# Strassen's scheme in the first half of layer 0 of a two-layer graph network

## The chip, the core and the metric

The kernel runs on one core of one Trainium2 chip. The metric is device time in microseconds for one execution. The kernel before takes 1528.7 us, the median of three runs (1527.5 to 1532.0).

The engines are called as in the profile: PE is TensorE (PEld its weight loads), DVE is VectorE, ACT is ScalarE, POOL is GpSimd, and SP is SyncE, which here only issues transfers. ACT and POOL issue transfers as well. Every engine takes its instructions in the order in which the program lists them.

## The reference

Two layers work on 2048 nodes, a batch of 8 and 64 features, all in fp32. Cut to what matters:

```python
# layer 0
w  = einsum('nd,dkio->nkio', embedding, weight)       # weights of each node
As = [I, A, 2*A@A - I]
x_g = einsum('knm,bmc->bnkc', stack(As), x)
x  = layernorm(x + einsum('bnki,nkio->bno', x_g, w) + b)
# layer 1: the same with supports I, A, 2*A@A - I and
apt = softmax(relu(E @ E.T), axis=1)
x  = layernorm(x + ...)
```

A is a dense 2048 x 2048 matrix. The products with A are computed as u = A x and then z = A u, on a right-hand side of 2048 rows and 8 x 64 = 512 columns. Each node has its own 64 x 64 weights, made from its embedding.

## The kernel before

The work is cut into 40 stages: five phases of eight blocks, a block being 256 nodes. Phase A0 makes u = A x for layer 0 and applies the weights to the features [x; u]. Phase B0 makes z = A u and ends layer 0 with its normalisation. A1, Z1 (the softmax support) and V1 do the same for layer 1. Stage n is block n mod 8 of phase n div 8, so A0 is stages 0 to 7, B0 stages 8 to 15, A1 stages 16 to 23.

A stage's own part is its product (`product`, line 410). All the rest is fed in between the product's matrix instructions: each `put(n, place, f, ...)` (line 657) says that f is to be issued in stage n at a place from 0 to 64, scaled to the stage's length (64 units for a plain stage, 56 for a Strassen stage). The loop at line 751 walks through the products and issues what has come due. So the order on each engine is written by hand, and a stage n + 1 carries work that belongs to stage n: making its weights on PE (`weights`, line 306, tiles `pw`, in bursts of two or three groups), copying them out of PSUM into `w` on ACT and DVE (`copy`), transposing u (`turn`, line 395, tile `pt`), applying the weights to the features (`apply`, line 327, tile `po`, followed by updates of `acc` on DVE), and storing the result (`post`, line 356).

Products come in two kinds. A plain one (`straight`, line 435, tile `pu`, in A0 and A1) streams the block's 256 rows of A in four pieces of 512 KB and issues 32 matrix instructions of 128 rows by 512 columns. A Strassen one (`strassen`, line 455, tiles `p1` to `p7`, shown as `p`) cuts the block's rows of A and the right-hand side into quarters and makes seven products of quarter size, eight matrix instructions of 256 columns each. Its left operands are three quarters of A and four sums of quarters (`lefts`, line 246); its right operands are three quarters of the right-hand side and four sums T1 to T4 of them (`Sums`, line 609), which DVE makes once in a phase.

Before the change, A0 is plain in all eight blocks, and B0, A1 and V1 are plain in block 0 alone (`plain`, line 215). While A0 runs, DVE makes the four sums of quarters of A for blocks 1 to 7 out of the streamed pieces (`sums_of_a`, line 555) and SP stores them to DRAM (`sd`); the later phases read them from there.

A0's u stays in `u_all` in SBUF, from where B0 reads it. The same room holds the raw first weights at the start (line 128), and in A1 the four right-hand sums T1 to T4.

Buffers that the change touches: `stream` has four buffers of 512 KB for pieces of A, filled in order by SP through `Ahead` (line 217), which asks for a new piece as soon as fewer than four are ready. There are two PSUM accumulators (`ps_acc`), handed out in turn, so a product can start once all readers of the product before the last are done. Three more PSUM tiles (`ps_big`) are handed out in turn to `pw`, `pb`, `pt` and `po`. `wst` (three buffers) holds split weights, filled by SP. `wraw`, `wsplit`, `sq` and `row` are single buffers with several users.

## Time and profile before

| | |
|---|---|
| median of three runs | 1528.7 us |
| the profiled execution's own time | 1533.8 us |
| its span, first to last instruction | 1532.0 us |
| PE busy | 1497.5 us |
| DVE busy | 889.3 us |
| ACT busy | 455.0 us |
| POOL busy | 184.4 us |
| moved by transfers | 274.95 MB, 179 GB/s on average |

In the profile's tables a group is written `out<-in`, by the program's names without buffer numbers, then its shape, its count, its busy time and the mean length of one instruction, and last the idle time of the engine just ahead of it with what ended that idle time. All lines of the kernel's own instructions are shown as L42, because one helper issues them; groups are told apart by their tiles. Every fp32 matrix instruction appears as two PE records. Records of PE overlap a little, so the mean length of one is longer than the distance between two; the chain of work, which counts each moment once, gives the distance.

### The profile page before, as it was taken

The page shows a single profiled execution, that of the slowest core. Times are in us where ns is not written, and L with a number is a line of the kernel's source. Part 1 is how long each engine was busy: PE and PEld are TensorE (multiplying, and loading weights), DVE is VectorE, ACT ScalarE, POOL GpSimd, SP SyncE. Part 2 cuts the span into 40 slices and gives each one's busy share as a digit, 9 for nine tenths or more (in the row PEclk, how much of TensorE's full clock was granted, in tenths as well). Part 3 has the DMA queues.
Part 4 walks back from the last instruction along what each step waited for, and adds up shares of the span by engine and source line. Part 5 has one row for each costly group of instructions (what it writes and reads, how often), then busy time and mean ns, then how long its engine had stood idle before and what let it go on. Part 6 is the DMA issues. An engine that isn't in the chain of part 4 may idle for free.

```text
span 1532.0 us, 30543 instructions
## 1 busy us (share of the span) xinstructions
PE 1497.5 (98%) x13114; PEld 1147.6 (75%) x13114; DVE 889.3 (58%) x1600; ACT 455.0 (30%) x578; POOL 184.4 (12%) x303
## 2 busy tenths in 40 slices
PE   8999999999999999989999999999999999999996
PEld 3444444457899999567777777788888888888885
DVE  2766666656566666766666666543433366666665
ACT  0333223222221112154444444411111133333332
POOL 4201011110111111111111111010000000000100
PEclk9999999999999999999999999999999999999998
DMA  9777787763576656588788877823211346665661
GB/s 347 240 240 212 234 253 249 230 219 115 179 224 226 196 192 199 157 152 210 192 168 192 207 206 202 166 79 100 66 38 42 88 131 195 196 198 194 197 197 51
DMA packets 93511, 274.95 MB, mean 179 GB/s; under 512 B 13632, under 2 KB 30016, under 8 KB 91776
## 3 DMA queue, kind: packets, MB, share of 16 engines
q1 hardware_dynamic: 65120, 180.38, 41.0%
q0 software_dynamic: 22784, 78.98, 17.9%
q10 hardware_dynamic: 5472, 13.63, 2.5%
q8 instruction: 104, 1.70, 0.4%
q14 instruction: 31, 0.25, 0.1%
HBM read 212.08 MB, written 56.64 MB: 175 GB/s over the span
## 4 chain that ended last, share of the span: by engine, by line
PE 77%; issue 14%; DMA 4%; DVE 3%; POOL 2%; ACT 0%; SPq 0%; POOLq 0%; ACTq 0%; DVEq 0%
PE p L42 24%; PE pz L42 18%; PE pu L42 13%; PE po L42 11%; PE pw L42 7%; PE pt L42 1%; DMA wst<-wd 1%; DMA x<-in_x 1%; PE ps L42 1%; DVE acc L42 1%; PE pr L42 1%; DMA u<-in_w 1%; DVE w L42 1%; POOL x1d L42 1%; POOL t L42 0%
## 5 line engine op out<-in xcount | busy, mean ns | idle before, releaser
L42 ACT ACTIVATE w<-pw 128x1024 f32<-128x1024 f32 x304 | 296.3, 1021 | 301.1 <-PE pw L42 301.0
L42 DVE SCALAR_TENSOR_TENSOR acc<-po,mask,acc 128x256 f32<-128x256 f32 (+1 forms) x640 | 247.2, 426 | 91.1 <-PE po L42 80.8
L42 DVE COPY w<-pw 128x1024 f32<-128x1024 f32 x144 | 176.2, 1224 | 188.5 <-PE pw L42 187.7
L42 PE MATMUL pu<-x,a 128*128 128x512 f32 x576 | 268.5, 609 | 5.8 <-DMA x<-in_x 3.4
L42 PE MATMUL pz<-p,x 128*128 128x256 f32 x1024 | 232.7, 380 | 0.0
L42 PE MATMUL p<-a,u 128*128 128x128 f32 x1792 | 219.4, 278 | 4.6 <-DVE temps L42 4.6
L42 PEld LDWEIGHTS p<-a,u 128*128 128x128 f32 x1792 | 206.5, 192 | 15.8 <-DVE temps L42 5.7
L42 PE MATMUL po<-w,t 128*32 128x256 f32 (+1 forms) x5120 | 207.6, 338 | 7.7 <-issue 4.1
L42 PEld LDWEIGHTS pz<-p,x 128*128 128x128 f32 x1024 | 189.3, 190 | 24.2 <-issue 0.6
L42 PEld LDWEIGHTS pu<-x,a 128*128 128x128 f32 x576 | 104.8, 192 | 121.5 <-issue 106.3
L42 PEld LDWEIGHTS po<-w,t 128*32 128x32 f32 (+1 forms) x5120 | 127.5, 108 | 83.6 <-issue 18.4
L42 PEld LDWEIGHTS pw<-e,wst 64*128 64x128 f32 x1728 | 112.0, 184 | 58.2 <-issue 35.4
L42 PE MATMUL pw<-e,wst 64*128 64x256 f32 x1728 | 145.8, 296 | 2.1 <-ACT w L42 1.1
L42 DVE SCALAR_TENSOR_TENSOR p<-ps,c 128x512 f32<-128x512 f32 x64 | 44.2, 691 | 120.4 <-PE ps L42 120.1
L42 PE MATMUL p<-u,a 128*128 128x256 f32 x448 | 112.3, 388 | 0.0
L42 ACT ACTIVATE p<-p 128x512 f32<-128x512 f32 x64 | 40.2, 630 | 181.9 <-DVE p L42 181.9
L42 PEld LDWEIGHTS p<-u,a 128*128 128x128 f32 x448 | 81.0, 190 | 16.2 <-issue 2.9
L42 PE MATMUL p<-a,x 128*128 128x128 f32 x672 | 84.7, 279 | 0.0
L42 PE MATMUL p<-x,a 128*128 128x256 f32 x336 | 81.2, 383 | 0.0
L42 PE MATMUL p<-a,w 128*128 128x128 f32 x672 | 81.1, 279 | 0.0
L42 PEld LDWEIGHTS p<-a,x 128*128 128x128 f32 x672 | 78.2, 192 | 3.7
L42 PEld LDWEIGHTS p<-a,w 128*128 128x128 f32 x672 | 78.2, 195 | 1.8 <-issue 1.6
(108 smaller groups left out, 1106.3 us busy)
## 6 DMA issues: line engine op xcount, KB each, us to landing
wst<-wd SPq DMA_DIRECT2D x108, 512.0 KB, 5.4
a<-sd SPq DMA_DIRECT2D x84, 512.0 KB, 6.2
a<-in_adj_q SPq DMA_DIRECT2D x63, 512.0 KB, 4.0
a<-in_adj_b SPq DMA_DIRECT2D x40, 512.0 KB, 6.3
sd<-sums SPq DMA_DIRECT2D x28, 512.0 KB, 3.3
bx<-bx POOLq DMA_DIRECT2D x32, 256.0 KB, 7.8
acc<-bx POOLq DMA_DIRECT2D x16, 512.0 KB, 5.9
pd<-acc POOLq DMA_DIRECT2D x16, 512.0 KB, 4.9
```

Source lines behind the costliest of these rows:

```text
L42: return self._tc.keep_in_program_order(f(*args, **kwargs))
```

## The change

In phase A0, blocks 2 to 7 are made with Strassen's scheme. Block 0 and block 1 stay plain.

The left operands of these six stages are made where they lie. The stage takes the four quarters A11, A22, A21 and A12 into the four `stream` buffers, holds them (`held`), and DVE writes each sum over a quarter that is no longer needed; a buffer is given back after p7, p6, p5 and p3. POOL stores each sum to `sd` for the later phases, in place of `sums_of_a` and SP's stores, which only block 1 keeps.

The seven products come in another order in all phases: p1, p4, p7, p2, p6, p5, p3 instead of p1, p2, p4, p6, p5, p7, p3, with two more additions on DVE.

The right-hand sums T1 to T4 for A0 are made in stage 1 in `u_all`. So u no longer stays there: each stage of A0 stores its u to DRAM (`ud`) from POOL, and SP loads it back into `u_all` at the end of stage 7 as the T's are used up, block 7 in stage 8.

Around these: the start loads 13 slabs of x instead of 10 ahead of the first raw weights and the last three ahead of the second; the first weight splits move to later places; the warm-up multiplies 7 times 128 columns instead of 5 times 512; raw weights are loaded into `sq` and split into `row`, at later places; in A0, two of 16 `w` copies go to DVE instead of five; B0's last two posts move a little; block 7's x is reloaded from one place; the last stage applies the weights in another order.

The diff, cut to its core:

```diff
-    for c, slabs in enumerate((range(10), range(10, 13), range(13, NJ), ())):
+    for c, slabs in enumerate((range(13), range(13, NJ), (), ())):
...
-    for _ in range(5):
-        pe.matmul(ps[:, 0, :], idle[:, 0:P], idle, start=True, stop=True)
+    for _ in range(7):
+        pe.matmul(ps[:, 0, 0:P], idle, idle, start=True, stop=True)
...
-    plain = {("A0", j) for j in range(NBLK)} | {(phase, 0) for phase in ("B0", "A1", "V1")}
+    plain = {("A0", 1)} | {(phase, 0) for phase in ("A0", "B0", "A1", "V1")}
...
-            while (len(self.ready) < self.bufs and self.order
+            while (len(self.ready) + self.held < self.bufs and self.order
...
+    lefts = [("quarter", (0, 0)), ("quarter", (1, 1)), ("sum", 2), ("quarter", (0, 1)), ("sum", 1), ("sum", 0), ("sum", 3)]
+    quarters = [("quarter", at) for at in ((0, 0), (1, 1), (1, 0), (0, 1))]
...
-                copy(0 if g % 3 == 1 else 1, dst, ps.rearrange("p h v n -> p n v h"))
+                copy(0 if g % (8 if self.phase == "A0" else 3) == 1 else 1, dst, ps.rearrange("p h v n -> p n v h"))
...
-            if self.phase == "A0":
-                self.slabs = U[SB * self.j:SB * self.j + SB]
+            if self.n == 0:
+                self.slabs = U[0:SB]
...
-            if self.phase == "A1":
+            if self.kk == 0:
                 for s in range(SB):
-                    sp.dma_start(out=ud[self.j][:, s, :], in_=self.slabs[s])
+                    (sp if self.li else pool).dma_start(out=ud[self.j][:, s, :], in_=self.slabs[s])
...
+            def quarter(name):
+                mine[name] = adj.next()
+                adj.held += 1
+
+            def sum_of_a(i, name, a, b, op):
+                dve.tensor_tensor(mine[name], mine[a], mine[b], op=op)
+                pool.dma_start(out=sd[self.j][i].rearrange("p k n -> p (k n)"), in_=mine[name])
...
+                if inside and name in ("p7", "p6", "p5", "p3"):
+                    adj.held -= 1
+                    adj.fill()
+                    self.used(what)
...
+            if inside:
+                quarter("A11")
+                quarter("A22")
+            yield from times("p1", "B11", "A11")
             act.copy(p1, made["p1"])
+            if inside:
+                quarter("A21")
+                sum_of_a(2, "A11", "A11", "A21", ALU.subtract)
+                sum_of_a(0, "A21", "A21", "A22", ALU.add)
+            yield from times("p4", "T4", "A22")
+            self.used("T4")
+            act.copy(p4, made["p4"])
+            if inside:
+                quarter("A12")
+                sum_of_a(1, "A22", "A22", "A11", ALU.subtract)
+            yield from times("p7", "T3", "A11")
+            add(v, made["p7"], p1)
+            add(p4, v, p4, ALU.subtract)
+            yield from times("p2", "B21", "A12")
             add((0, 0), made["p2"], p1)
+            if inside:
+                sum_of_a(3, "A12", "A12", "A22", ALU.subtract)
+            yield from times("p6", "T2", "A22")
+            add(v, made["p6"], v)
+            add(p1, made["p6"], p1)
+            add((1, 0), made["p6"], p4)
+            yield from times("p5", "T1", "A21")
+            add(p1, made["p5"], p1)
+            add((1, 1), made["p5"], v)
             self.repeat(1)
+            yield from times("p3", "B22", "A12")
+            add((0, 1), made["p3"], p1)
...
+        def used(self, what):
+            first = {"T4": 0, "T1": 4, "T2": 8, "T3": 12}.get(what)
+            if (self.phase, self.j) == ("A0", NBLK - 1) and first is not None:
+                load_u(range(first // 2, min(first // 2 + 2, NBLK - 1)))
...
-    for c, (n, places) in enumerate(((0, (14, 16, 18)), (0, (26, 28, 30)), (0, (38, 40, 42)), (0, (48, 50, 52)))):
+    for c, (n, places) in enumerate(((0, (40, 42, 44)), (0, (50, 52, 54)), (0, (58, 60, 62)), (1, (2, 4, 6)))):
...
-        put(1 + n, 56, load_weights, *key)
+        put(2 + n, 4, load_weights, *key)
         for part in range(3):
-            put(2 + n, 18 + 5 * part, split_weights, part, *key)
+            put(2 + n, 24 + 5 * part, split_weights, part, *key)
...
+    for i, place in enumerate((16, 24, 30, 52)):
+        put(1, place, sums["A0"].make, i)
+    put(8, 2, load_u, (NBLK - 1,))
...
-                bursts, posts = (19, 19, 29, 29), (37, 41, 45)
+                bursts, posts = (19, 19, 29, 29), (38, 42, 48)
...
-    for i, place in ((2, 59), (3, 62)):
-        put(len(stages) - 1, place, last.apply, i)
+    put(len(stages) - 1, 60, last.apply, 2)
...
-    last.post(0, 8, 16)
-    last.apply(0)
-    last.post(1, 8, 16)
-    last.apply(1)
+    for c in (3, 0, 1):
+        last.apply(c)
+        if c == 0:
+            last.post(0, 8, 16)
+            last.post(1, 8, 16)
```

More of the change, by code (lines that the diff above doesn't have):

```diff
@@ L116, in load_weights @@
         part = slice(8 * c, 8 * c + 8)
-        a = room[0] if room else one.tile([P, 8, P], F32, tag="wraw", name="wraw")
+        a = room[0] if room else one.tile([P, 8, P], F32, tag="sq", name="wraw")
         act.dma_start(out=a, in_=layers[li][1][kk][:, part, :])
@@ L136, in two_graph_layers @@
         raw.append((e, b))
-    idle = one.tile([P, BC], F32, tag="wsplit", name="idle")
+    idle = one.tile([P, P], F32, tag="wsplit", name="idle")
     dve.memset(idle, 0.0)
     ps = big("pi")
-    for _ in range(5):
-        pe.matmul(ps[:, 0, :], idle[:, 0:P], idle, start=True, stop=True)
+    for _ in range(7):
+        pe.matmul(ps[:, 0, 0:P], idle, idle, start=True, stop=True)
     ident = const.tile([P, P], F32, tag="ident", name="ident")
@@ L180, in split_weights @@
                 dve.tensor_scalar(twice, twice, 2.0, None, op0=ALU.mult)
-            s = room() if room else one.tile([P, 8, P], F32R, tag="wsplit", name="wsplit")
+            s = room() if room else one.tile([P, 8, P], F32R, tag="row", name="wsplit")
             dve.tensor_copy(s, a)
@@ L206, in two_graph_layers, with load_u @@
     cd = [dram.tile([2, SB, P], F32, tag=f"cd{j}", name=f"cd{j}") for j in range(NBLK)]
+    def load_u(blocks):
+        for j in blocks:
+            sp.dma_start(out=u_all[:, 2 * j:2 * j + 2, :], in_=ud[j])
     def rows_of(t):
@@ L221, in __init__ @@
             self.bufs, self.new, self.load, self.written = bufs, new, load, written
-            self.order, self.ready = list(order), []
+            self.order, self.ready, self.held = list(order), [], 0
         def fill(self):
-            while (len(self.ready) < self.bufs and self.order
+            while (len(self.ready) + self.held < self.bufs and self.order
                    and (self.written is None or self.order[0] in self.written)):
@@ L243, in load_adj @@
             sp.dma_start(out=t, in_=src.rearrange("p k n -> p (k n)"))
-    lefts = [("quarter", (0, 0)), ("quarter", (0, 1)), ("quarter", (1, 1)),
-             ("sum", 1), ("sum", 0), ("sum", 2), ("sum", 3)]
+    lefts = [("quarter", (0, 0)), ("quarter", (1, 1)), ("sum", 2), ("quarter", (0, 1)), ("sum", 1), ("sum", 0), ("sum", 3)]
+    quarters = [("quarter", at) for at in ((0, 0), (1, 1), (1, 0), (0, 1))]
     adj = Ahead(4, lambda: stream.tile([P, 4 * NB], F32, tag="a", name="a"), load_adj,
@@ L250, in two_graph_layers @@
                  for key in ([("plain", j, i) for i in range(NJ // 4)] if (phase, j) in plain
-                             else [(kind, j, i) for kind, i in lefts])])
+                             else [(kind, j, i) for kind, i in (quarters if phase == "A0" else lefts)])])
     wst = Ahead(3, lambda: three.tile([P, 8, P], F32R, tag="wst", name="wst"),
@@ L385, in post @@
                 pool.dma_start(out=rows_of(x1d[self.j][s0 * P:s1 * P, :]), in_=a)
-                if g < GROUPS:
-                    self.load_x(range(s0 * SB // GROUPS, s1 * SB // GROUPS))
         def load_x(self, slabs):
@@ L463, in strassen, with times @@
             temps = one.tile([P, 4, half], F32, tag="wsplit", name="temps")
-            p1, p4, u2, u4 = (temps[:, i, :] for i in range(4))
-            made = {}
-            def times(name, what):
+            p1, p4, v = (temps[:, i, :] for i in range(3))
+            made, mine = {}, {}
+            inside = self.phase == "A0"
+            def quarter(name):
[4 more added lines that the diff above has]
+                pool.dma_start(out=sd[self.j][i].rearrange("p k n -> p (k n)"), in_=mine[name])
+            def times(name, what, left):
                 made[name] = acc = self.accumulator(name)[:, 0:half]
-                a = adj.next().rearrange("p (k n) -> p k n", n=P)
+                a = (mine[left] if inside else adj.next()).rearrange("p (k n) -> p k n", n=P)
                 for k in range(k_slab):
@@ L490, in add @@
                         dve.tensor_tensor(to[:, :, 4 * dst[1] + par:4 * dst[1] + par + 3:2], of(a), of(b), op=op)
-            yield from times("p1", "B11")
+            if inside:
+                quarter("A11")
+                quarter("A22")
+            yield from times("p1", "B11", "A11")
             act.copy(p1, made["p1"])
-            yield from times("p2", "B21")
-            add((0, 0), made["p2"], p1)
-            yield from times("p4", "T4")
-            act.copy(p4, made["p4"])
-            yield from times("p6", "T2")
-            add(u2, made["p6"], p1)
-            yield from times("p5", "T1")
-            add(u4, made["p5"], u2)
-            yield from times("p7", "T3")
-            add(u2, made["p7"], u2)
-            add((1, 1), made["p7"], u4)
-            add((1, 0), u2, p4, ALU.subtract)
+            if inside:
[12 more added lines that the diff above has]
+            yield from times("p2", "B21", "A12")
+            add((0, 0), made["p2"], p1)
+            if inside:
[7 more added lines that the diff above has]
+            add((1, 1), made["p5"], v)
             self.repeat(1)
-            yield from times("p3", "B22")
-            add((0, 1), made["p3"], u4)
+            yield from times("p3", "B22", "A12")
+            add((0, 1), made["p3"], p1)
             self.repeat(0)
             self.store_u()
+        def used(self, what):
+            first = {"T4": 0, "T1": 4, "T2": 8, "T3": 12}.get(what)
+            if (self.phase, self.j) == ("A0", NBLK - 1) and first is not None:
+                load_u(range(first // 2, min(first // 2 + 2, NBLK - 1)))
         def repeat(self, s):
@@ L638, in two_graph_layers @@
         r = thirds(room, n)
-        sums[phase] = Sums(slabs, r if n == 4 else [r[0], None, r[1], r[2]])
+        sums[phase] = Sums(slabs, [r[1], r[2], r[3], r[0]] if n == 4 else [r[0], None, r[1], r[2]])
+    sums["A0"] = sums["A1"]
     stages = [Stage(8 * i + j, phase, j) for i, phase in enumerate(("A0", "B0", "A1", "Z1", "V1"))
@@ L688, in two_graph_layers @@
     for j in range(NBLK):
-        put(24 + j, 12, lambda j: sp.dma_start(out=u_all[:, 2 * j:2 * j + 2, :], in_=ud[j]), j)
+        put(24 + j, 12, load_u, (j,))
     for n, st in enumerate(stages):
@@ L696, in two_graph_layers @@
         if phase == "A0":
-            for c in range(NJ // 4 if st.j else 0):
+            for c in range(NJ // 4 if st.j == 1 else 0):
                 put(n, 16 * c + 10, st.sums_of_a, c)
@@ L704, in two_graph_layers @@
                 bursts, posts = (6, 6, 12, 12), ()
+                put(n + 1, 26, st.load_x, range(SB))
                 for k in range(6):
```

## The prediction

> **What bounds the kernel now.** I read the page's sections 1, 2 and 5 first, then the chain of work that ended last, then the order of instructions on TensorE (PE) and VectorE (DVE) around the places the change touches.

> From the page:

> ```profile
> PE 1497.5 (98%) x13114; PEld 1147.6 (75%) x13114; DVE 889.3 (58%) x1600; ACT 455.0 (30%) x578; POOL 184.4 (12%) x303
> PEclk9999999999999999999999999999999999999998
> L42 PE MATMUL pu<-x,a 128*128 128x512 f32 x576 | 268.5, 609 | 5.8 <-DMA x<-in_x 3.4
> ```

> PE is busy 98% of 1532.0 us at full clock, and hardly anything else holds it. So time comes from PE work removed, or from its few waits. `pu` is the plain product A·X. It has 576 records, two per matrix instruction: eight stages of layer 0 and one of layer 1, at 64 records each.

> The chain through one whole layer-0 stage (start us, us, what), and the same stretch of a layer-1 stage that already uses the seven products:

> ```profile
> 108.92 7.04 PE po L42 x128
> 115.96 12.21 PE pu L42 x28
> 128.18 0.90 PE pw L42 x11
> 129.08 2.77 PE pu L42 x6
> 131.85 0.91 PE pw L42 x12
> 132.75 2.77 PE pu L42 x6
> ...
> 150.91 0.33 PE po L42
> ```
> ```profile
> 690.99 7.04 PE po L42 x128
> 698.03 1.92 PE p L42 x8
> 699.96 0.87 PE pt L42 x8
> 700.83 3.46 PE p L42 x16
> 704.29 0.46 PE pr L42 x2
> 704.75 1.29 PE p L42 x6
> ...
> 732.38 2.71 PE po L42 x45
> ```

> Both stages are PE from end to end: 41.98 us plain, 41.39 us with seven products although that one also holds `pr` and a second `pt`. An undisturbed `pu` record takes 12.21/28 = 0.436 us, a 256-column `p` record 3.46/16 = 0.216 us. 64 × 0.436 = 27.9 us against 7 × 8 × 2 × 0.216 = 24.2 us.

> The first stage does wait (PE in order of time; the bracket is the idle time before):

> ```profile
> 32.80 8.89 PE L42 MATMUL pu<-x,a 128*128 128x512 f32 x16 [3.38 <-DMA x<-in_x]
> 47.31 0.74 PE L42 MATMUL pw<-e,wsplit 64*128 64x256 f32 x8 [1.52 <-DVE w L42]
> 52.01 0.50 PE L42 MATMUL pw<-e,wsplit 64*128 64x256 f32 x4 [0.29 <-DVE bx L42]
> ```

> And its clock dips there (columns: stretch, PE, PEld, DVE, ACT, POOL busy, granted clock, DMA share, GB/s):

> ```profile
> 30.00:35.00 5.00, 2.20 (x3) 0.76 (x4) 3.82 (x4) 1.28 (x1) 0.00 (x0) 0.77 1.03 404
> 35.00:40.00 5.00, 5.00 (x11) 2.29 (x12) 1.77 (x3) 0.60 (x1) 0.00 (x0) 0.89 0.90 346
> ```

> [...] So the seven products cost 7/8 here too, less restart losses. [...] the trace's 128x1024 `acc` subtraction takes 1225, and its 128x2048 sums 2286.

> **The change, part by part.**

> *Six layer-0 stages (blocks 2 to 7).* The new stage is the layer-1 stage without `pr` and one `pt`. In 41.39 us the chain holds po 7.04, six pw bursts 4.97, pr 1.86, pt 1.74, pb 0.14, leaving 25.64 for the products: 24.2 plus restarts after other work. New stage: 25.64 + 7.04 + 4.97 + 0.14 + 0.9 = 38.7 us. Gain 41.98 − 38.7 = 3.3 us, six times: **−19.8 us**.

> Costed at nothing, with the cover (times from the stage's first product, laid out with these durations):
> - Quarter sums: 4 × 1.225 = 4.9 us of DVE instead of 16 × 0.42 = 6.7. The one that matters is A11−A21: p1 ends at 5.7, the sum at 6.9, p7 needs it at 10.2. A21 is requested when p5 of the stage before ends, 9 us ahead of p1's end; quarters land in 4.0 us (median).
> - Their stores go on POOL (0.55 us issue each, engine 12% busy). The next A11 load waits for that store and p7's end (15.7). Queued behind it on SP are only a weight refill and later quarters, whose first use is after 38.7.
> - Nine adds of 0.42 instead of seven. p3 reuses p6's bank, freed by three adds behind the 7.9 us of `acc` updates: DVE is done at 33.3, p3 starts at 35.4.
> - Fourteen of 16 `w` copies on ACT: 0.95 us each in a row, three per burst, bursts 3.2 us apart; p1's copy comes 2.5 us before p7 needs the bank. This and the `t` copies (done 21.1, po at 22.1) are the thinnest slacks, about 1 us. If a cover fails, that excess is paid in each of six stages.
> - Raw weights are now loaded at the stage's start into the buffer of the A sums, from ACT. In stage 2 that issue waits for the last A-sum store (I place it at 85, ACT being free at 84); behind it stand the `w` copies of burst 2, due at 85. Under 1 us once, taken as 0.
> - u through DRAM: 4 MB each way. POOL's store stands after the stage's last add, ahead of the next sum's store, which is due 6 us later; the u buffer is written again only after p2, 21 us on, against 17.4 us for the slowest such store in layer 1. Traffic per stage goes from 229 GB/s to my estimate of 260; the trace has slices of 347.

> *Start.* Three x slabs move ahead of the first weight chunk, and the last three pass the second: 0.75 MB less before slab 13. From about 2 us on the ACT queue lands 5.0 MB by 32.8, 0.16 MB/us, so x13 comes some 4 us earlier; if all engines share the freed 0.75 MB at 375 GB/s it is 2. Stage 0 then ends near 35.5–37.5 instead of 40.3. Next is DVE: two later weight splits of 3.9 us each, then the first `w` copy, at about 42.3 instead of 46.0, as the last split now stands behind it. Five operand-sum instructions of 2.29 us enter stage 1 on DVE, three `w` copies leave it. In program order from 42.3: w copy 1.2, last split 3.9, A sums 1.7, bias 1.3, T1 2.3, w copy 1.2, T2 2.3, A sums 1.7, bias 1.3, T3 2.3, `t` copies 1.4: 62.9. The first po needs those copies and starts near 63 instead of 66.9. **−4.0 us**, bounds −2 and −6. Shorter warm-up matmuls: bounds −1.5 (PE starts at the first tile)[...]; taken as 0, since slab 13 sets the end.

> *Layer 0's second half starts.* Block 7's u is stored by POOL and loaded by SP at once; SP blocks meanwhile, and the fourth weight refill stands behind it. Add 0.4, two issues 1.1, landing 4–8, load issue 0.4, refill landing 5.4–7: 12–17 us after the last product; needed at 352.4 − 337.1 = 15.3. Bounds 0 and 2.5: **+0.5**.

> *Other phases.* The B0 stages wait 0.77 us each for DVE before p3:

> ```profile
> 480.77 5.18 PE L42 MATMUL p<-a,u 128*128 128x128 f32 x44 [0.77 <-DVE temps L42]
> ```
> In the new order p3 waits for p6's three adds behind two of the three normalisation steps: (0,0) adds to 474.0, mean and subtraction to 476.7, square on ACT and its sum to 479.1, adds to 480.8: the same moment. 0, bounds ±3 over six. Layer 1's products keep over 1 us of slack at p3. The x reload of stage 16 moves from two places to one; its store still waits for DVE at 646.7: 0, bounds −1.5 and +1.

> *Tail.* PE waits 2.15 us for DVE's `t` add, since an `acc` update stands ahead. Moving that apply behind the product fills the wait, but DVE is then the bound (three applies and two steps, last update 1523.2 instead of 1523.8): **−0.6**.

> Sum: −19.8 − 4.0 + 0.5 − 0.6 = −23.9. The profiled execution took 1533.8 us, span 1532.0: predicted span 1508, own time 1510. The median of the runs is 1528.7, 5 lower: **1505**.

> **Rivals.**
> 1. *A new wait in each of the six stages.* Speaking for it: 1 us slacks, DVE in order, landings up to 14 us for the stored sums. 1 to 2.5 us per stage gives back 6 to 15: 1511–1520. Against: DVE busy only 26.5 of 42.0 us in a stage now.
> 2. *The start gives more.* Removing the stall also removes the clock dips (0.77 and 0.89 between 30 and 40 us), and stage 16 or B0 gain: −4 to −8 more, 1497–1501. Against: the DVE backlog in stage 1.
> 3. *Slower.* The in-place buffers serialise: A21 can be requested only when p5 of the stage before has read its buffer, 3.5 us before the stage. p7 (due 10.2, after a sum of 1.25) stands still once A21 lands more than 12.4 us after its request. Stages 3 to 7 then lose the excess each (stage 2's quarters are fetched during stage 1): at 17 us the gain is gone, from 18.5 us on the time is 1505 + 5 × 6.1 = 1535 and more. Against: 4.0 us is the median for quarters; 14 us occurs for stored sums as a single maximum.
> 4. *The products don't shorten the stage* because DVE becomes its bound at 42 us: about 1525. Against: DVE's 26.5 us in a stage now, less A sums 6.7, three `w` copies 3.7 and a u copy 0.7, plus 4.9 and 3.8, is 24.

> **Chances.** As worked out, 1501–1509: 0.62. Rival 1: 0.17. Rival 2: 0.14. Rival 3: 0.04. Rival 4: 0.03. Likeliest 1505. From 1497 to 1514 lie the first case, most of rival 2 and a third of rival 1, together 0.8. A measurement here can't tell less than 0.3% (4.6 us) from no change: faster 0.93 (the first case, rivals 1 and 2), same 0.03 (rival 4), slower 0.04 (rival 3).

> **What would show it.** Right: `pu` down to 192 records; po to po 38–39 us in stages 3 to 7 with PE unbroken; first po near 63; 1.2 us `a` sums on DVE never named ahead of a `p`. Wrong: PE waits on `DVE a`, `DMA a<-in_adj_q` or `ACT w` recurring every 38 us; first po still at 66; a wait on `wst<-wd` some 15 us into the first B0 stage; B0 waits above 0.8.

## The result, and the profile after

The changed kernel takes 1506.4 us (median of four runs, 1505.9 to 1507.7), against 1528.2 for the kernel before in the same series (1527.5 to 1532.0). The ratio is 0.9854, with a 95% interval of 0.9836 to 0.9871. The prediction said 1505.0, between 1497 and 1514.

The profiled execution after took 1506.8 us with a span of 1505.0, so the two spans differ by 27.0 us where the medians differ by 21.8: the profiled execution of before lay 5.6 us above its median, the one of after 0.4. The page of the kernel after, in the lines that answer to those shown of before, and the line for the queue that carries instructions:

```profile
PE 1472.4 (98%) x13406; PEld 1200.7 (80%) x13406; DVE 895.1 (59%) x1599; ACT 475.6 (32%) x608; POOL 206.6 (14%) x343
q8 instruction: 106, 1.74, 0.5%
L42 PE MATMUL pu<-x,a 128*128 128x512 f32 x192 | 91.5, 624 | 1.8 <-DMA x<-x1d 1.8
```

PE still sets the time. `pu` is down from 576 records to 192, three plain stages, while PE has 292 records more in all: the smaller products are more numerous. The chain of work that ended last, in one new stage (start us, us, what):

```profile
179.72 7.04 PE po L42 x128
186.77 10.13 PE p L42 x46
196.89 0.90 PE pw L42 x12
197.80 2.79 PE p L42 x12
...
216.20 2.16 PE p L42 x10
218.36 3.79 PE po L42 x65
```

From `po` to `po` it is 38.64 us without a wait on PE, where the plain stage took 41.98. Set side by side by such landmarks, the two profiles divide the 27.0 us as follows:

| stretch | before | after | difference | predicted |
|---|---|---|---|---|
| start of span to first `po` | 66.9 | 62.2 | -4.8 | -4.0 |
| six stages and what lies between (stage 1 `po` to stage 8 `po`) | 293.7 | 273.6 | -20.1 | -19.8 |
| stage 8 `po` to stage 17 `po` (all of B0, start of A1) | 330.3 | 329.8 | -0.5 | +0.5 |
| stage 17 `po` to last full `po` | 781.9 | 781.5 | -0.3 | 0 |
| last full `po` to end | 59.2 | 57.9 | -1.3 | -0.6 |

The start still waits, by PE in order of time (the bracket is the idle time before), and loses clock. The fourth line is busy time by stretch (PE, PEld, DVE, ACT, POOL, then granted clock, DMA share, GB/s):

```profile
40.45 0.82 PE L42 MATMUL pw<-e,wsplit 64*128 64x256 f32 x8 [2.06 <-DVE w L42]
41.20 3.54 PE L42 MATMUL pu<-x,a 128*128 128x512 f32 x4
47.24 0.50 PE L42 MATMUL pw<-e,wsplit 64*128 64x256 f32 x4 [0.75 <-DVE bx L42]
```
```profile
41.00:44.40 3.40, 3.40 (x9) 1.51 (x5) 3.31 (x5) 1.93 (x2) 0.00 (x0) 0.50 0.19 74
```

Product 0 no longer waits for x. PE waits instead for the first `w` copy on DVE (39.17 to 40.40 us), which stands behind the third weight split (35.2 to 39.1), and just after that wait the clock is halved for 3.4 us: four `pu` records take 3.54 us, where four take 1.96 at full clock in the same stage.

In B0 there is something that the prediction did not have. PE in order of time:

```profile
440.06 1.59 PE L42 MATMUL po<-w,t 64*32 64x128 f32 x96 [1.09 <-issue]
452.60 5.15 PE L42 MATMUL p<-a,u 128*128 128x128 f32 x44 [0.70 <-PE p L42]
474.42 1.72 PE L42 MATMUL po<-w,t 64*32 64x128 f32 x101 [0.85 <-issue]
```

The 0.70 us ahead of p3 is the old wait of 0.77, as predicted. (The view names PE itself as what ended it; on DVE p6's additions end at 452.5 us, queued behind the sum of the square, which ends at 451.0.) There are more of the waits called "issue", most of them inside the dense `po` bursts: in stages 8 to 16 they sum to 6.56 us after and 3.71 before. What they are is the main question of the experiments.

### The profile page after: what moved, and what is told of

It is laid out like the page before. It is cut to its first block, busy times and chain, and to the rows that moved or that the text cites. A ratio compares the mean times of both kernels' runs of the same rounds, so it can differ in the third digit from the quotient of the medians.

```text
span 1505.0 us, 31332 instructions
## 1 busy us (share of the span) xinstructions
PE 1472.4 (98%) x13406; PEld 1200.7 (80%) x13406; DVE 895.1 (59%) x1599; ACT 475.6 (32%) x608; POOL 206.6 (14%) x343
## 3 DMA queue, kind: packets, MB, share of 16 engines
q8 instruction: 106, 1.74, 0.5%
## 4 chain that ended last, share of the span: by engine, by line
PE 75%; issue 17%; DVE 3%; POOL 2%; DMA 2%; ACT 1%; POOLq 0%; ACTq 0%; DVEq 0%
PE p L42 34%; PE pz L42 18%; PE po L42 10%; PE pw L42 8%; PE pu L42 2%; DMA x<-in_x 1%; PE pt L42 1%; PE ps L42 1%; PE pr L42 1%; DVE acc L42 1%; DVE w L42 1%; POOL x1d L42 1%; DMA u<-in_w 1%; POOL t L42 1%; DVE wsplit L42 1%
## 5 line engine op out<-in xcount | busy, mean ns | idle before, releaser
L42 ACT ACTIVATE w<-pw 128x1024 f32<-128x1024 f32 x328 | 318.3, 1021 | 369.6 <-PE pw L42 366.8
L42 DVE SCALAR_TENSOR_TENSOR acc<-po,mask,acc 128x256 f32<-128x256 f32 (+1 forms) x640 | 247.0, 427 | 83.7 <-PE po L42 71.0
L42 PE MATMUL pz<-p,x 128*128 128x256 f32 x1024 | 232.7, 380 | 0.0
L42 DVE COPY w<-pw 128x1024 f32<-128x1024 f32 x120 | 146.9, 1224 | 139.4 <-PE pw L42 138.2
L42 PE MATMUL p<-a,u 128*128 128x128 f32 x1792 | 219.4, 278 | 4.4 <-PE p L42 4.1
L42 PEld LDWEIGHTS p<-a,u 128*128 128x128 f32 x1792 | 206.6, 192 | 15.2 <-PE p L42 5.1
L42 PE MATMUL po<-w,t 128*32 128x256 f32 (+1 forms) x5120 | 206.1, 337 | 7.3 <-issue 6.3
L42 PEld LDWEIGHTS pz<-p,x 128*128 128x128 f32 x1024 | 189.3, 190 | 24.2 <-issue 0.6
L42 PE MATMUL p<-u,a 128*128 128x256 f32 x832 | 203.6, 387 | 0.0
L42 PEld LDWEIGHTS po<-w,t 128*32 128x32 f32 (+1 forms) x5120 | 125.8, 108 | 81.2 <-issue 15.4
L42 PEld LDWEIGHTS p<-u,a 128*128 128x128 f32 x832 | 152.0, 190 | 29.7 <-issue 5.4
L42 PE MATMUL p<-x,a 128*128 128x256 f32 x624 | 152.6, 385 | 0.0
L42 PE MATMUL pw<-e,wst 64*128 64x256 f32 x1728 | 146.0, 296 | 1.2 <-ACT w L42 1.1
L42 PEld LDWEIGHTS pw<-e,wst 64*128 64x128 f32 x1728 | 112.1, 184 | 41.8 <-issue 21.6
L42 PEld LDWEIGHTS p<-x,a 128*128 128x128 f32 x624 | 114.2, 190 | 19.0 <-issue 0.7
L42 DVE SCALAR_TENSOR_TENSOR p<-ps,c 128x512 f32<-128x512 f32 x64 | 44.3, 691 | 119.6 <-PE ps L42 119.1
L42 ACT ACTIVATE p<-p 128x512 f32<-128x512 f32 x64 | 40.1, 629 | 181.5 <-DVE p L42 181.5
L42 PE MATMUL pu<-x,a 128*128 128x512 f32 x192 | 91.5, 624 | 1.8 <-DMA x<-x1d 1.8
L42 PE MATMUL p<-a,x 128*128 128x128 f32 x672 | 83.0, 278 | 0.1
L42 PE MATMUL p<-a,w 128*128 128x128 f32 x672 | 81.3, 277 | 0.0
L42 PEld LDWEIGHTS p<-a,x 128*128 128x128 f32 x672 | 77.8, 192 | 3.0 <-issue 0.2
L42 PEld LDWEIGHTS p<-a,w 128*128 128x128 f32 x672 | 77.3, 192 | 2.5 <-issue 1.4
```

What stands on the lines that cost most here:

```text
L42: return self._tc.keep_in_program_order(f(*args, **kwargs))
```

## The experiments

Every time below is a median. Runs of one group share runs of the kernel before, and each ratio is to those.

### Parts of the change alone

The kernel before once more, the change with blocks 1 to 4 plain (three Strassen stages instead of six; the sums of A of the plain ones are made in smaller buffers), the kernel before with only the new order of the seven products and what follows from it, and the kernel before with only the edits to its two ends (the order of the first loads and splits, the warm-up, the last stage's order), with block 7's x reloaded from one place.

```diff
-    plain = {("A0", 1)} | {(phase, 0) for phase in ("A0", "B0", "A1", "V1")}
+    plain = {("A0", j) for j in (1, 2, 3, 4)} | {(phase, 0) for phase in ("A0", "B0", "A1", "V1")}
```

> The kernel before once more, for a second profile. Its profiled execution took 1533.8 us, 5 above the median of its runs, while the changed kernel's lies on its median. Theory: one or two places with waits that come and go (the 2.43 us gap in po in the first B0 stage, and the start), so this profile is 3 to 6 us shorter and lacks them, and the six layer-0 stages of 41.98 us are the same. Rival: the whole program runs slower in that execution, then stages differ by 0.3% everywhere.

> The changed kernel with blocks 2, 3 and 4 of phase A0 plain again (their sums of A made as for block 1, in smaller buffers); blocks 5 to 7 stay seven products. Theory (the gain is the shorter stage, 3.35 us each): 3 x 3.35 = 10 us slower than the changed kernel, 1516.4 us, with 41.98 us from po to po in those stages and 38.6 in the others. Rival (most of the gain is at the start, the ends or in the order of the products): less than 4 us slower, under 1510.

> The kernel before with the new order of the seven products (and its two more additions and the moved posts) in B0, A1 and V1 alone. Theory: the order by itself changes nothing: 1528 us, within 2, B0 stages still waiting 0.7 us before p3. Rival 1: it brings part of the gain, 1524 or less. Rival 2: it costs in B0, where the changed kernel's stages were 0.9 us longer than before (34.5 instead of 33.6): 1532 to 1534.

> The kernel before with the changes at its ends alone: x slabs first, short warm-up, later weight splits, one place for block 7's x, and the last stage's order of applies. Theory: first po 5 to 7 us earlier (no operand sums on DVE here), stage 16 0.5, tail 1.2: 1521 to 1522 us. Rival: DVE, which makes the weights, swallows the earlier x: 1525 or more.

Kernel before, a single run: 1532.9 us, so it did not come out shorter as expected. The 27 runs of the kernel before in that group range from 1526.3 to 1533.1, and the first B0 stage of this one again holds an "issue" wait of 2.48 us. The spread belongs to the kernel before; both profiled executions of it lie in its upper part.

Three plain stages: 1516.9 us, ratio 0.992 (0.990 to 0.994); expected 1516.4. `po` to `po` is 41.9 us in its plain stages and 38.6 in its Strassen ones. The term for the six stages holds in both halves.

Order alone: 1534.7 us, ratio 1.004 (1.002 to 1.006), 4.7 us slower than before, where my theory had no change. The wait ahead of p3 did not grow; "issue" waits did:

```profile
437.76 0.94 PE L42 MATMUL po<-w,t 64*32 64x128 f32 x48 [0.42 <-issue]
449.47 5.15 PE L42 MATMUL p<-a,u 128*128 128x128 f32 x44 [0.53 <-PE p L42]
```

They sum to 9.07 us against 3.71 in the kernel before. The profiled execution took 1540.1 us, 5.5 over the median of its eight runs, so its waits are more than the usual loss: from stage 8 `po` to stage 17 `po` it takes 337.4 us instead of 330.3, of which 4.8 are these waits and 1.7 one more half-clock stretch, at 632 us. My rival 2 (a price in B0, 1532 to 1534) came nearest: the new order does cost there, and it isn't a wait on DVE.

Ends alone: 1527.6 us, ratio 0.9989 (0.9981 to 0.9996); expected 1521 to 1522. The tail gained its 1 us. The start gained nothing: the first `po` is at 66.8 us, as before. Most of what its profile is shorter by lies where the edits were not aimed: from stage 8 `po` to stage 17 `po` it takes 323.9 us instead of 330.3, with 1.17 us of "issue" waits instead of 3.71 and without the half-clock stretch at 394 us. DVE and then PE at the start, in order of time:

```profile
39.80 0.69 DVE L42 TENSOR_TENSOR u<-u 128x512 f32<-128x512 f32 x1 [1.60 <-DMA u<-in_w]
43.74 1.23 DVE L42 COPY w<-pw 128x1024 f32<-128x1024 f32 x1
```
```profile
45.02 1.22 PE L42 MATMUL pw<-e,wsplit 64*128 64x256 f32 x8 [5.96 <-DVE w L42]
```

Slab 13 of x comes earlier and product 0 ends earlier, as worked out, and PE then waits 5.96 us for the `w` copy behind the third split. That split itself waited for its raw weights, which DVE had by 35.2 us in the changed kernel. The traces show a difference on POOL. In the changed kernel POOL waits for u until 30.9 us, to store it, and only then issues the load of `t` (34.9 us) and the store of the first split weights (35.4 us). With the ends alone there is no u to store; POOL issues these two at 22.7 and 29.8 us, in the midst of the raw weights. From 24 to 30 us POOL's queue (q0) then moves 0.59 MB instead of 0.13, ACT's (q10), which brings the raw weights, 1.12 instead of 1.55, and the third chunk has landed at 39.7 us instead of 34.5. So the earlier start of the changed kernel seems to come from the order on POOL, which the change altered for another reason; no run tests this alone.

### Is the slack of the first sum real?

```diff
                 dve.tensor_tensor(mine[name], mine[a], mine[b], op=op)
+                for _ in range(2 if i == 2 else 0):
+                    dve.tensor_tensor(mine[name], mine[name], mine[b], op=ALU.add)
+                    dve.tensor_tensor(mine[name], mine[name], mine[b], op=ALU.subtract)
```

> The change with the sum A11-A21 followed by two pairs of an addition and a subtraction of A21 over the same buffer, so that the first left sum of stages 2 to 7 takes five DVE instructions of 1.2 us instead of one, and is ready 4.9 us later; the output's last bits differ. The prediction costs this sum at nothing because it is ready 3.3 us before p7 needs it (6.9 against 10.2 us into the stage). Theory: p7 then waits 4.9 - 3.3 = 1.6 us, up to 2.5 with the copies and adds queued behind it: +10 to +15 us over six stages, 1516 to 1521. Rival 3 would have the buffers themselves late already (A21's landing, not the sum, ends p7's slack): +25 us or more. If nothing moves, the slack was over 4.9 us and my layout of the stage was wrong.

1523.2 us, 17 more than the change. Each of stages 2 to 7 now waits ahead of p7 (PE in order of time; one of six, 1.89 to 1.92 us each):

```profile
136.98 0.67 PE L42 MATMUL p<-u,a 128*128 128x256 f32 x2 [1.92 <-DVE a L42]
```

Four instructions of 1.22 us add 4.9, of which 1.9 shows: the slack is 3.0 us, predicted 3.3. Once, at 95.3 us, the half clock follows such a wait. I had expected 10 to 15 us more: between stage 1 `po` and stage 8 `po` the profile takes 14.4 more, 1.7 of them by that half clock, and the start of this execution takes 1.9 more (first `po` at 64.0 us). The buffers were not late, so rival 3 falls.

### The waits called "issue"

The page counts 106 packets and 1.74 MB on the instruction queue. PE's list in the trace has 27,218 entries (13,406 products, as many weight loads, 406 others). 1.74 MB over 27,218 is 64 bytes each, so a packet of 16 KB would be 256 of PE's entries. The times agree: from the packet that starts at 340.9 us to the one at 610.3, 31 packets later, PE passes 8,012 entries, 258 for each. I counted, for each "issue" wait on PE of all fourteen profiles, the place in PE's list of the record that ended it, modulo 256:

```
kernel                            at 192 or 193: waits, us    elsewhere: waits, us (place)
before                              2   3.71                  1   0.42 (201)
before, again                       3   3.68                  1   0.42 (201)
after                               8   6.56                  -
three plain stages                  7   3.93                  -
order alone                        10   9.07                  -
ends alone                          1   1.17                  1   0.19 (213)
longer first sum                    8   5.70                  -
later posts                         8   4.46                  -
16 tiny products more              12  14.64                  -
start splits moved                  7   5.38                  1   0.78 (147)
loads moved                         7   7.35                  -
loads moved, 16 tiny products more 12  15.32                  -
posts, splits, loads                6   4.71                  1   0.78 (147)
posts, splits, x load               7   4.10                  1   0.78 (147)
```

98 of 104 stand at the same place of 256. The decisive run shifts the list and changes nothing else:

```diff
     for _ in range(7):
         pe.matmul(ps[:, 0, 0:P], idle, idle, start=True, stop=True)
+    for _ in range(16):
+        pe.matmul(ps[0:32, 1, 0:32], idle[:, 0:32], idle[:, 0:32], start=True, stop=True)
```

> The change with 16 more tiny warm-up products (32 columns by 32) ahead of the first product, 32 records of products and 32 of weight loads; from there on PE's instructions are the same, each 64 later in its list. The po bursts of stages 9 to 14 hold one gap each, after records 92, 96, 101, 105, 110, 114 of 128 in the changed kernel. Theory: PE runs out of fetched instructions at a fixed spot of its list (its instructions come in packets of 16 KB on a queue of their own). Then the gaps come 32 product records earlier in the bursts, near 60, 64, 69, 73, 78, 82, and everything else stays; the time moves by at most 2 us either way. Rival: the gaps belong to something that the burst itself waits for (a bank, a transfer, a semaphore that the trace misses): they stay near 92 to 114.

The waits moved. PE in order of time, where the same bursts had 96 and 101 records after their wait:

```profile
442.72 2.01 PE L42 MATMUL po<-w,t 64*32 64x128 f32 x127 [0.89 <-issue]
446.83 0.27 PE L42 MATMUL po<-w,t 64*32 64x128 f32 x1 [2.10 <-issue]
478.85 0.71 PE L42 MATMUL p<-a,u 128*128 128x128 f32 x5 [1.12 <-issue]
482.41 0.41 PE L42 MATMUL po<-w,t 64*32 64x128 f32 x5 [0.94 <-issue]
```

My expectation misread such rows: the 92 to 114 are the records that follow a wait, not those ahead of it. Of 128 records, 96 following becomes 127 following, so the wait comes 31 or 32 records earlier, which is what the theory said; in the next stage it comes 5 product records ahead of the burst. The size was wrong, though: I gave the shift at most 2 us, and it costs 11.5 (1517.8 us; ratio 0.9936, 0.9921 to 0.9951). Most stages now hold two waits instead of one, 14.64 us instead of 6.56. From stage 8 `po` to stage 17 `po` the profile takes 340.2 us instead of 329.8: 8.1 us are these waits, and 1.7 a half-clock stretch behind one of them. The first `po` is at 62.2 us as before, so the tiny products themselves cost nothing.

The waits are tied to the packets in time too. Over the 87 such waits of at least 0.25 us between 340 and 640 us in the fourteen profiles, the wait ends 2.5 us (2.2 to 2.8) after the latest packet starts to move. So in these profiles a wait is long when its packet starts late. The kernel with the order alone shows that the place is not all: its list stands at the same places as that of the kernel before (p3 of stage 10 is entry 6616 in both), yet in the `po` bursts of stages 10 to 12 its packets start 1.6 to 3.8 us after PE passes the spot before, those of the kernel before 0.9 to 1.7.

Do they stand behind the data? Two loads were issued later in the program order, once on the changed kernel and once on the shifted one:

```diff
-                put(n + 2, 5, st.load_x, range(SB))
+                put(n + 2, 5 if st.j == 6 else 42, st.load_x, range(SB))
...
-            put(*((1, 26) if n == 0 else (n, 48 + 6 * st.li) if st.kk == 0 else (n, 30)), st.load_acc)
+            put(*((1, 26) if n == 0 else (n, 48 + 6 * st.li) if st.kk == 0 else (n, 42 if phase == "B0" and st.j < 7 else 30)), st.load_acc)
```

> The change with two of B0's transfers issued later: the load of acc from place 30 to 42 (stages 8 to 14), and that of x from place 5 to 42 of the stage after next (but for block 6). In the changed kernel 3 MB of loads of SP and POOL are issued between 426 and 432 us, ahead of the po bursts of stage 10; they drain at 437.5, and only then does the 16 KB packet of PE's instructions start that ends the gap of 1.09 us at 440.06. Theory: the packet stands behind the data, so with 1 MB of it moved behind the bursts it starts earlier, and the gaps of stages 9 to 14 (0.19 to 1.64 us, 5.6 in all) shrink to under 2 us in all: the time falls by 3 to 5 us, to 1501 to 1503. Rival: the packet is asked for at a fixed time after a spot of the list and doesn't mind the traffic: the gaps stay, 1505 to 1508.

> The same two moves on top of the kernel with 16 tiny products more (1517.8 us, 14.6 us of gaps in stages 8 to 14, two in each stage). Theory (the packets stand behind data): at least the half of it goes, 1508 to 1511. Rival (the traffic doesn't matter, only the spot): 1516 to 1519.

1507.2 and 1518.3 us: nothing gained. But these two runs do not answer the question, since the loads did not move in time. POOL in order of time in the first of these two kernels, from the moment the store of `x1d` has landed:

```profile
427.69 1.13 POOL L42 DMA_DIRECT2D x<-x1d  x2 [2.53 <-DMA x1d<-acc]
428.81 0.53 POOL L42 DMA_DIRECT2D acc<-pd  x1
431.75 1.06 POOL L42 DMA_DIRECT2D e<-ed  x2 [2.40 <-PE pw L42]
```

A place in the plan only orders the instructions of POOL; between the old place and the new one POOL waits for nothing, so it issues at the same moment. A third run, told of below, put the wait of the next store between; there the load of x leaves the stretch, and the waits still sum to 4.10 us against 4.71. In it the packet of stage 10 starts at 432.9 us, 3.8 us after the spot before, in the midst of transfers of some 375 GB/s; so it did not stand until all data had drained. But four loads land between 432.4 and 433.6 us, so a link to the data is not excluded. What makes a packet start late stays open.

### The known waits, and a better kernel

B0's last two posts later, so that p6's additions no longer stand behind the square and its sum on DVE:

```diff
-                bursts, posts = (19, 19, 29, 29), (38, 42, 48)
+                bursts, posts = (19, 19, 29, 29), (38, 46, 50)
```

> The change with B0's last two normalisation steps 4 places later (about 3 us), so that p6's three additions no longer stand behind the square and its sum on DVE. My theory of the p3 wait (0.70 us in each of stages 9 to 15, the adds queued behind the steps): the wait on DVE ahead of p3 is gone in six or seven stages, and the time falls by 4 us to about 1502. Rival: PE stands still as long for something else in the same stage (the gaps inside the po bursts that the trace puts down to nothing grow, or acc updates of the next po come late): no gain, 1505 to 1508.

1505.0 us (1503.9 to 1505.4). The waits ahead of p3 are gone in all stages, which shows what they were, and from stage 8 `po` to stage 17 `po` the profile takes 326.0 us instead of 329.8, the 4 us expected. The median gained only 1.4, and the span 1.7: in the profiled execution the start is 1.7 us longer, since the half-clock stretch lies at 48.4 us in it, behind the wait on `bx`. In the changed kernel it lies at 41.0, ahead of that wait, which shrinks from 2.4 to 0.75 us in return.

The third and fourth weight splits later, the third behind the first `w` copy:

```diff
-    for c, (n, places) in enumerate(((0, (40, 42, 44)), (0, (50, 52, 54)), (0, (58, 60, 62)), (1, (2, 4, 6)))):
+    for c, (n, places) in enumerate(((0, (40, 42, 44)), (0, (50, 52, 54)), (1, (2, 4, 6)), (1, (13, 15, 17)))):
```

> The change with the third weight split moved from stage 0 (places 58 to 62) to stage 1 (2 to 6), and the fourth from there to (13 to 17): the first w copy on DVE no longer stands behind the third split, nor the first bias add behind the fourth. Theory: the start is bound by DVE's order there: the waits of 2.06 us (for the first DVE w copy) and 0.75 us (for bx) go, the first po starts at 59.5 to 60 instead of 62.15, and the time falls by 2 to 2.5 us. Rival: another of the start's steps is right behind (the last t copies at 61.87, or DVE itself, now with the splits behind the bias): the first po stays within 0.7 us of 62.15.

1503.1 us (1502.8 to 1506.0). In this form the last chunk of layer 0's first weights and the first stored one changed places in their queue, so these weights are applied to the wrong features; the work is the same. PE in order of time:

```profile
38.83 0.97 PE L42 MATMUL pw<-e,wsplit 64*128 64x256 f32 x12
44.01 0.51 PE L42 MATMUL pw<-e,wsplit 64*128 64x256 f32 x4 [0.54 <-DVE bx L42]
```

The wait on `w` is gone, no half clock follows, and the first `po` is at 60.0 us instead of 62.15: the 2 us expected. The medians can't tell either of these two kernels from the change: their ratios are 0.9851 (0.9836 to 0.9866) and 0.9844 (0.9829 to 0.9859), against 0.9854 (0.9836 to 0.9871). What each gains is read from its stretch of the profile.

All of it together, the weight stores moved behind the splits (places 19 to 31 of stage 1) so that the chunks keep their order:

> The two moves of loads, the later posts of B0 and the later third and fourth weight splits together on the changed kernel, with the first weight stores at places 19 to 31 of stage 1 so that the chunks keep their order. If the three are independent: 1506.4 - 1.4 (posts) - 3 (start) - 4 (loads) = 1498. If they share one cause (the gaps grow where a wait goes): 1501 to 1503.

1501.3 us (1500.1 to 1504.4), ratio 0.9812 (0.9791 to 0.9834), some 5 us under the change. With the load of `acc` back at its place and that of x for blocks 0 to 4 behind the next store:

> The kernel with the later posts and splits, with the load of acc back at place 30 and that of x (for blocks 0 to 4) behind the next store of x1d (place 52 of the stage after next). The two moves in the runs before did not move these loads in time: POOL issued them at 427.7 and 428.8, right behind the store that it stands at, as before (425.8 and 426.9), since between the places nothing on POOL waits. Here the store's wait stands between, so 0.5 MB of the 3 MB leaves the stretch ahead of the po bursts. Theory (the instruction packets stand behind the data): the packets of stages 10 to 14 start about 1.3 us earlier and their gaps (0.46 to 1.09 us) fall to 0.3 or less; 2 to 3 us, 1498 to 1499.5. Rival (the traffic doesn't matter): gaps as before, 1500 to 1502.5.

1502.0 us (1500.1 to 1503.9), ratio 0.9818 (0.9804 to 0.9833): no better, and within the noise the same. Since the loads gained nothing in their own run, what the two gain on the change is the posts and the splits. In the first of them, the lowest median of all, "issue" waits still cost 4.71 us.

## Why the prediction was right, point by point

**The length of a product.** The sum uses what the trace of before shows, 436 and 216 ns a record. In a new stage of the changed kernel the first 46 `p` records take 10.13 us, 220 ns each. The sums of A on DVE took the 1.225 us (median of 21) that the prediction had put in.

**Six layer-0 stages, -19.8.** Right: -20.1. The stage was put at 38.7 us and is 38.63. PE waits for nothing in them, so all that was costed at nothing was hidden. The slack of the first sum was measured at 3.0 us for 3.3. Rival 1 (a new wait in each stage) and rival 4 (DVE at its bound) did not occur.

**Start, -4.0.** The size is right, and the named bound too: DVE's splits and copies, not x. The -4.8 is one of the better cases: in the six other profiles with this start the first `po` starts at 62.2 us once and at 63.7 to 64.2 five times, so about -3 is more usual. In the sum the first `w` copy was put at 42.3 us; it began at 39.2 (46.0 before), but of these 3 us only 0.8 arrived at the first `po`. Two things were missed. One is that the edits of the start alone give nothing: the third chunk of raw weights came earlier only in the changed kernel, with POOL's other transfers behind it. It also has fewer `w` copies on DVE, and no run separates the two. The other is the clock: here a wait of PE of 2.06 us is followed by a half-clock stretch, in which four `pu` records take 1.58 us more than at full clock. I had this in rival 2, as a gain when the stall goes; part of the stall stayed, and so did one stretch.

**Layer 0's second half starts, +0.5.** No wait at all: SP issued block 7's load at 320.9 us and the weight refill right behind it. Within the bounds given (0 to 2.5).

**Other phases, 0.** Here the step failed in its reason, and that its sum is near is luck. The wait ahead of p3 stayed as said, 0.70 us. But the list of PE's instructions was not on my account: 2.9 us more of waits for instructions in stages 8 to 16. They were paid back by waits of the profiled execution of before that the changed one did not have: one half-clock stretch (1.7 us; the one behind the 2.43 us wait of the first B0 stage), `u` on ACT 0.87, x 0.62, `wst` 0.58, `t` 0.37 and 0.44 in six stages ahead of p3. All of this makes -1.7 against -0.5 found; 1.2 us over nine stages stay unassigned. A shift of the list by 64 entries would have cost 11.5 us more, and 1517.8 lies outside the predicted range.

**Tail, -0.6.** -1.3: PE's wait of 2.15 us for `t` is gone and the last update of `acc` comes 1.3 us earlier, relative to the last full `po`.

**The step from span to median.** The sum was made against an execution 5 us over its median, and the difference was taken off as it stood. Part of what was counted as the kernel's waits was that execution's own, and so the spans differ by 27.0 us and the medians by 21.8. The predicted -23.9 lies between. That the forecast of 1505 came within 1.4 us is in part luck: the profiled execution was put at 1510 and took 1506.8, and the 5 us taken off it to reach the median were 0.4. The two errors cancel.

## What to carry to other kernels

Where an engine is busy 98% and a product is replaced by a smaller one, the gain can be read from a stage of the same kernel that already runs the smaller one, less what it does besides; it came out at a tenth of a microsecond per stage. Then look at the waits that the profile assigns to nothing, and number them in the engine's own list: where they stand at equal distances, suspect the supply of instructions, and shift the list with a few idle instructions: here 16 of them moved the waits by 31 or 32 records of the burst. And a transfer moved to a later place of its queue moved in time here only where something on that engine waits between the two places: without a wait between, POOL issued the loads of x and `acc` at 427.69 and 428.81 us, right behind the store it waits for, as in the changed kernel (425.83 and 426.95); with the wait of the next store between, the load of x left the stretch.

## What the runs showed of the hardware that was not expected

PE's own instructions cost time in these runs. In bursts of short matrix instructions (128 `po` records and as many weight loads in 2.03 us) PE stands still at places that lie whole multiples of 256 entries apart in its list (98 of 104 waits), 0.19 to 2.43 us at a time in the kernels before and after, and resumes about 2.5 us after a 16 KB packet starts. Sixteen idle products, ahead of everything, cost 11.5 us of 1506; 8.1 of these are such waits in the profile.

Some waits of PE cost twice in these runs. Tail aside, the half-clock stretches in the traces last 3.41 us, or twice that. Over the fourteen profiles, tail and first 15 us aside, such a stretch began in, or up to 1.6 us after, 22 of 26 waits of 2.2 us and more, 5 of 17 waits of 1.85 to 2.2, and 2 of 69 waits of 0.8 to 1.85 us. Each 3.41 us at a granted clock of 0.50 cost up to 1.7 us; in the one at 41 us of the changed kernel, four `pu` records took 3.54 us instead of 1.96.
